# Summing in-degrees beside a bitonic merge sort instead of after it, in a two-part graph network

## The chip, the cores and the metric

The kernel runs on one NeuronCore of a Trainium2 chip. The engines that matter are TensorE (PE, matmuls; its weight loads are the row PEld), VectorE (DVE), ScalarE (ACT), GpSimd (POOL) and the queues that issue DMAs (SP above all). Each has its own stream of instructions and they meet only at semaphores. The metric is the device time of one execution in microseconds (us).

## The reference, cut to what matters

A graph of 12,500 nodes and 412,500 edges (an edge list sorted by destination) goes through a two-layer graph convolution and then through a mesh network with two message steps. The convolution needs, for every node, the sum of the weights of the edges that end in it:

```python
def _gcn_conv(x, row, col, edge_w, W, b, num_nodes):
    ...                                   # self loops of weight 1 are added to row, col, edge_w
    deg = jax.ops.segment_sum(ew, c, num_segments=num_nodes)
    dis = jnp.where(deg > 0, jax.lax.rsqrt(deg), 0.0)
    norm = dis[r] * ew * dis[c]
    msg = (x @ W.T)[r] * norm[:, None]
    return jax.ops.segment_sum(msg, c, num_segments=num_nodes) + b

x = _layernorm(x + gcn2(relu(gcn1(x))))
x = _layernorm(x + mesh_gnn(x, edge_attr, src, dst))   # two steps of edge and node networks
```

`deg` is what this case is about. The mesh network also needs the plain number of edges into each node, so the kernel sums two rows at once: the weights and ones.

## The kernel before

The edges lie in 405 groups of K = 8 columns of 128 edges. Since they are sorted by destination, all destinations of a group fall in a window of W = 64 nodes that starts at the group's first destination, `base_row[g]`. A sum over a group is therefore eight small matmuls: a one-hot of 128 edges by 64 places, times a 128 by 2 tile `wt` of weights and ones, added up in PSUM to a 2 by 64 result, which DVE then adds to the row pair `deg` at the place `base_row[g]`. That place is read by DVE's sequencer from memory into a register before each addition (`values_load`).

The program has these stages, in order of time:

1. Preparation (to 79 us): destinations relative to the groups' bases go to DRAM as `rel_d`; edge lists are loaded.
2. The sort (79 to 792 us). Each of 128 partitions holds a row of RL = 3328 edges and sorts it by source, so that the convolution can later read its table in order. It is a merge network of 78 stages (`stage`, two nested loops over p and c). In a stage, `exchange` (lines 234 to 241) gives DVE three two-input operations over up to 1664 pairs, L237 (a mask of who is larger, written to PSUM), L238 (minimum) and L239 (maximum), and then two predicated copies of the carried weights, L240 and L241. Stages with a remainder have two or three such sets; there are 104 in all. ACT copies the weights over first (L248) and copies the keys that a stage doesn't touch (L244). PE and POOL do nothing here.
3. The sorted rows are split into parts and turned by PE (792 to 822 us).
4. The in-degrees (822 to 1267 us): `edge_loop` runs three times over 135 groups. Per group DVE builds the whole one-hot (128 by 512) in one operation (L385), PE does the eight matmuls (L397), DVE loads the place (L401) and adds (L405). The result is written to DRAM (L691) and read back in another shape (L695) for the reciprocal square root.
5. Two rounds of messages of the convolution (to 4890 us), then the mesh network (to the end), where POOL gathers rows by indirect DMAs.

`spread_degrees` and other `spread_` functions are a slow path for graphs whose windows are wider; for this graph their loops run zero times, at the price of the loop's entry alone. Where `manual_schedule` is used, instructions stay in the order in which they are written; elsewhere a planner sets the order on each engine.

Of the kernel before, what the change touches and what calls it, by code (L numbers as in the profile page):

```python
# [9 lines left out]
F32 = mybir.dt.float32  # L10
I32 = mybir.dt.int32
BF16 = mybir.dt.bfloat16
AF = mybir.ActivationFunctionType
OP = mybir.AluOpType
AX = mybir.AxisListType
ET = mybir.EngineType

NP = 125
P = 128
K = 8  # L20
W = 64
D = 64
GB = 135
SI, DR = 81, 45
R, LA = 5, 3
GI = 5
# [11 lines left out]
def gcn_then_mesh_gnn_kernel(ctx: ExitStack, tc: tile.TileContext, a: dict, out: bass.AP):  # L38
# [23 lines left out]
    NB = N // NP  # L62
    NT = a["dstT"].shape[1]
    NG = NT // K
    TB, IT = GB * K, NG // GB
    TI, ITS = GI * K, NG // GI
    NACC = N + NR
    CB = 4
    NCH = NB // CB
    CN = CB * NP  # L70
    KP = K // 2
    assert N == NB * NP and NB == NCH * CB and NT == IT * TB == ITS * TI

    dram = ctx.enter_context(tc.tile_pool(name="dram", bufs=1, space=bass.MemoryType.DRAM))
    const = ctx.enter_context(tc.tile_pool(name="const", bufs=1))
# [62 lines left out]
    nc.vector.memset(ones, 1.0)  # L138
    base_row = const.tile([1, NG], I32, name="base_row")
    span_row = const.tile([1, ITS], I32, name="span_row")  # L140
    trips = const.tile([1, 6], I32, name="trips")
    rbase_row = const.tile([1, NR], I32, name="rbase_row")
    x1 = const.tile([NP, NB, F], F32, name="x1")

    with tc.tile_pool(name="prep", bufs=2) as prep:
        ldst = prep.tile([P, NT], I32, name="ldst", bufs=1)
        nc.sync.dma_start(ldst, a["dstT"])
        for g0 in range(0, NG, P):
            n = min(P, NG - g0)
            gi = prep.tile([P, K * P], I32, name="gi")  # L150
            nc.sync.dma_start(gi[:n], a["dstG"][g0:g0 + n, :])
            gf = prep.tile([P, K * P], F32, name="gf")
            nc.vector.tensor_copy(gf[:n], gi[:n])
            st = prep.tile([P, 3], F32, name="st")
            nc.vector.tensor_reduce(st[:n, 0:1], gf[:n], axis=AX.X, op=OP.min)
            nc.vector.tensor_reduce(st[:n, 1:2], gf[:n], axis=AX.X, op=OP.max)
            nc.vector.tensor_sub(st[:n, 2:3], st[:n, 1:2], st[:n, 0:1])
            nc.sync.dma_start(base_f[g0:g0 + n, :], st[:n, 0:1])
            nc.sync.dma_start(span_f[g0:g0 + n, :], st[:n, 2:3])

            gr = prep.tile([P, 2, KP, P], BF16, name="gr")
            nc.vector.tensor_scalar(gr[:n].rearrange("g h j e -> g j h e"),
                                    gf[:n].rearrange("g (j h e) -> g j h e", h=2, e=P),
                                    st[:n, 0:1], None, op0=OP.subtract)
            nc.sync.dma_start(relg_d[g0:g0 + n].rearrange("g h c -> g (h c)"),
                              gr[:n].rearrange("g h j e -> g (h j e)"))
        base_bc = prep.tile([P, NG], F32, name="base_bc", bufs=1)
        nc.sync.dma_start(base_bc, base_f.rearrange("g o -> o g").to_broadcast([P, NG]))
        rows = prep.tile([1, 2, NG], F32, name="rows", bufs=1)
        nc.sync.dma_start(rows[:, 0, :], base_f.rearrange("g o -> o g"))  # L170
        nc.sync.dma_start(rows[:, 1, :], span_f.rearrange("g o -> o g"))
        nc.vector.tensor_copy(base_row, rows[:, 0, :])
        mspan = prep.tile([1, ITS], F32, name="mspan", bufs=1)
        nc.vector.tensor_reduce(mspan, rows[:, 1, :].rearrange("o (i g) -> o i g", g=GI),
                                axis=AX.X, op=OP.max)
        nc.vector.tensor_scalar_add(span_row, mspan, 1.0)

        most = prep.tile([1, 1], F32, name="most", bufs=1)
        tf = prep.tile([1, 4], F32, name="tf", bufs=1)

        mins = prep.tile([1, NCH, 2], F32, name="mins", bufs=1)
        nc.gpsimd.iota(mins[:, :, 1], pattern=[[CN, NCH]], base=CN, channel_multiplier=0,
                       allow_small_or_imprecise_dtypes=True)
        nc.vector.memset(mins[:, :, 0], float(N))
        for c in range(NCH):
            if last_group[c] < NG - 1:
                nc.vector.tensor_reduce(mins[:, c:c + 1, 0], rows[:, 0, last_group[c] + 1:], axis=AX.X, op=OP.min)
        nc.vector.tensor_tensor(mins[:, :, 0], mins[:, :, 0], mins[:, :, 1], op=OP.is_ge)
        held = prep.tile([1, 1], F32, name="held", bufs=1)
        nc.vector.tensor_reduce(held, mins[:, :, 0], axis=AX.X, op=OP.min)  # L190
        nc.vector.tensor_reduce(most, rows[:, 1, :], axis=AX.X, op=OP.max)
        nc.vector.tensor_scalar(tf[:, 0:1], most, float(W), held, op0=OP.is_lt, op1=OP.mult)
        nc.vector.tensor_scalar(tf[:, 2:3], tf[:, 0:1], -1.0, 1.0, op0=OP.mult, op1=OP.add)
        nc.vector.tensor_scalar_mul(tf[:, 1:2], tf[:, 2:3], float(ITS))
        nc.vector.tensor_scalar_mul(tf[:, 3:4], tf[:, 0:1], float(IT))
        nc.vector.tensor_copy(trips[:, 0:2], tf[:, 0:2])
        nc.vector.tensor_copy(trips[:, 4:6], tf[:, 2:4])
        dstrel = prep.tile([P, NT], F32, name="dstrel", bufs=1)
        nc.vector.tensor_copy(dstrel, ldst)
        rel3 = dstrel.rearrange("p (g k) -> p g k", k=K)  # L200
        nc.vector.tensor_tensor(rel3, rel3, base_bc[:, :, None].to_broadcast([P, NG, K]), op=OP.subtract)
        nc.sync.dma_start(rel_d, dstrel)
# [7 lines left out]
    with tc.tile_pool(name="sort", bufs=1) as sp, \  # L210
# [1 line left out]
        keys = [sp.tile([NR, RL], F32, name=f"key{i}") for i in range(2)]  # L212
        vals = [sp.tile([NR, RL], F32, name=f"val{i}") for i in range(2)]
        st = sp.tile([NR, 3], F32, name="rst")
        ki = sp.tile([NR, RL], I32, name="ki")
        kj = sp.tile([NR, RL], I32, name="kj")
        mask = pp.tile([NR, RL // 2], I32, name="mask")
        k, other = keys

# [71 lines left out]
            for move in moves:  # L291
                move()

        p, turn = 1, 0
        while p < RL:
            c = p
            while c:
                stage(p, c, keys[turn], keys[1 - turn], vals[turn], vals[1 - turn])
                turn, c = 1 - turn, c // 2
            p *= 2  # L300
        k, free = keys[turn], keys[1 - turn]
        tiles = lambda t: t.rearrange("r (j e) -> r j e", e=P)

# [38 lines left out]
        for t, to in ((free, slot_t), (k, drel_t), (vals[turn], ew_t)):  # L342
            for j0 in range(0, NS, 4):
                n = min(4, NS - j0)
                pt = pp.tile([128, 512], F32, name="ps_st", bufs=2)
                for j in range(n):
                    nc.tensor.transpose(pt[:, j * NR:(j + 1) * NR], tiles(t)[:, j0 + j, :], ident)
                nc.scalar.copy(to[:, j0:j0 + n, :], pt[:, :n * NR].rearrange("e (j r) -> e j r", r=NR))
# [34 lines left out]
    def one_hot(pool, drl, g):  # L383
        oh = pool.tile([P, K, W], F32, name="oh")
        nc.vector.tensor_tensor(oh, iow[:, None, :].to_broadcast([P, K, W]),  # L385
                                drl[:, g * K:(g + 1) * K, None].to_broadcast([P, K, W]), op=OP.is_equal)
        return oh
# [31 lines left out]
    def trip_count(i, most):  # L419
        return nc.values_load(trips[0:1, i:i + 1], min_val=0, max_val=most,  # L420
                              skip_runtime_bounds_check_because="all or none")

    def edge_loop(pool, body):

        with tc.For_i(0, trip_count(5, IT)) as it:
            drl = pool.tile([P, TB], F32, name="drl", bufs=1)
            nc.sync.dma_start(drl, rel_d[:, ds(it * TB, TB)])
            offs = pool.tile([1, GB], I32, name="offs")
            nc.vector.tensor_copy(offs, base_row[0:1, ds(it * GB, GB)])
            body(it, drl, offs)  # L430

    def spread_loop(pool, body, acc, r0, m, which=1):

# [71 lines left out]
    with tc.tile_pool(name="gcn", bufs=1) as gp, tc.tile_pool(name="gcnw", bufs=2) as gw:  # L505
# [19 lines left out]
        nc.sync.dma_start(w2t, a["W2T"])  # L525
        b1 = column(gp, "b1", a["L0_gnn_b1"])
        b2 = column(gp, "b2", a["L0_gnn_b2"])
        nc.vector.memset(deg, 0.0)

        def weights(pool, it, n):  # L530
            ew = pool.tile([P, n], F32, name="ew")
# [3 lines left out]
        def weights_and_ones(pool, it, n):  # L535
            wt = pool.tile([P, n, 2], F32, name="wt")
            nc.vector.tensor_copy(wt[:, :, 0], weights(pool, it, n))
            nc.vector.memset(wt[:, :, 1:2], 1.0)
            return lambda t: [wt[:, t, :]]

        def degrees(it, drl, offs):
            val = weights_and_ones(dw, it, TB)
            for g in range(GB):
                window_sum(one_hot(dw, drl, g), offs, g, lambda k: val(g * K + k), deg, 0, 2)

        with tc.tile_pool(name="degrees", bufs=2) as dw:
            edge_loop(dw, degrees)

        def weigh(xg, ew, g):
            nc.vector.tensor_mul(xg, xg, ew[:, g * K:(g + 1) * K, None].to_broadcast([P, K, F]))  # L550
# [102 lines left out]
                    fold_up(*folds.pop(0))  # L653

        def spread_degrees():
            with tc.tile_pool(name="spread", bufs=2) as sw:
                def body(it, group):
                    val = weights_and_ones(sw, it, TI)
                    for g in range(GI):
                        group(g, val)  # L660
                    return val

                spread_loop(sw, body, deg, 0, 2)

        def spread_messages(table):
            with tc.tile_pool(name="spread", bufs=2) as sw:
# [21 lines left out]

        spread_degrees()

        nc.sync.dma_start(deg_d, deg[:, :2 * NBK * P])  # L691
        by_block = lambda row: row.rearrange("o (b p) -> (o b) p", p=P)
        d = gp.tile([2 * NBK, P], F32, name="d")
        pos = gp.tile([2 * NBK, P], F32, name="pos")
# [618 lines left out]
```

## Time and profile before

| | us |
|---|---|
| median of 15 runs | 15397.31 |
| lowest and highest of them | 15358.05, 15450.96 |
| the profiled execution, its own time | 15461.96 |
| its span | 15460.2 |
| the sort in it | 79 to 792 |
| the in-degrees in it | 822.5 to 1267.5 |

The profile is of one execution, 65 us above the median of the runs. Its page gives busy time by engine; "idle before" is how long the engine stood still just ahead of an instruction, with what ended it. The share of busy time over the whole span says little here, since the stages have different limits; each has to be read for itself. Records of POOL are rough. A small letter q behind an engine's name marks its sequencer, which loads registers, waits and issues DMAs while the engine itself may be busy.

### The profile page before, as it was taken

The numbers are of one execution on the slowest core, as the hardware profiler recorded it, in microseconds if no ns is written. First come the engines' busy times: TensorE is split into PE (matmuls) and PEld (weight loads), VectorE is DVE, ScalarE is ACT, GpSimd is POOL, SyncE is SP. The second block draws the span as 40 slices with busy tenths as digits, with TensorE's granted clock in tenths as the row PEclk, the third lists the DMA queues.
The fourth block names the chain that finished last, engine by engine and source line by source line (L and its number), as shares of the span: only waits on it lengthen the run. The fifth ranks groups of instructions, "written<-read, shape, count | busy, mean of one in ns | idle before, by whom it ended". The sixth has DMA issues, their size and how long they took to land. (4 is left out here: it accounts for less than half of the span.)

```text
span 15460.2 us, 272960 instructions
## 1 busy us (share of the span) xinstructions
PE 11395.6 (74%) x104538; PEld 8580.0 (55%) x104539; DVE 8750.2 (57%) x22373; ACT 2375.2 (15%) x3731; POOL 6370.9 (41%) x6741
## 2 busy tenths in 40 slices
PE   0089999999998788888888888885655556565565
PEld 0078999789997455555455555553444444444443
DVE  9977777677777455555455455453444444444444
ACT  3400000000001222222222222221111111111111
POOL 0000000000001555556565556555666666666664
PEclk9999999899997688888788878787777777777777
DMA  0001111121111222222222222222222222222222
GB/s 28 0 15 54 66 66 66 48 69 66 65 65 47 57 60 61 59 60 62 56 61 60 58 60 62 56 60 58 60 60 60 60 61 60 61 61 60 60 59 50
DMA packets 958543, 871.49 MB, mean 56 GB/s; under 512 B 599416, under 2 KB 706192, under 8 KB 956548
## 3 DMA queue, kind: packets, MB, share of 16 engines
q1 hardware_dynamic: 258034, 493.54, 9.7%
q0 software_dynamic: 207360, 212.75, 7.8%
q10 hardware_dynamic: 491796, 147.08, 4.1%
q8 instruction: 859, 14.07, 0.4%
q14 instruction: 494, 4.05, 0.1%
HBM read 718.12 MB, written 134.51 MB: 55 GB/s over the span
## 5 line engine op out<-in xcount | busy, mean ns | idle before, releaser
L415 POOL DMA_INDIRECT pg<-tab_p,si x6480 | 6277.9, 969 | 3973.9 <-issue 1698.8
L1052 PE MATMUL ps_o<-eb_w,h 128*128 128x128 f32 x6480 | 1381.2, 380 | 1850.2 <-ACT h L1045 1640.2
L1052 PEld LDWEIGHTS ps_o<-eb_w,h 128*128 128x128 f32 x6480 | 1176.1, 272 | 2107.7 <-ACT h L1045 1778.1
L607 PE MATMUL ps_h<-t,roh 128*128 128x112 bf16 (+1 forms) x39936 | 2132.1, 211 | 65.9 <-DVE roh L583 65.9
L607 PEld LDWEIGHTS <-roh 128*128 128x128 bf16 x39936 | 2011.3, 98 | 115.3 <-issue 112.0
L789 POOL MEMSET zero<- 64x192 bf16 x1 | 0.3, 251 | 4015.9 <-DVE agg L639 4015.9
L1116 DVE TENSOR_SCALAR ot<-rb,iop 128x512 bf16<-128x512 bf16 x810 | 294.3, 363 | 2359.0 <-DMA rb<-relg_d 1482.3
L623 PE MATMUL ps_seg<-ohd,msg 128*112 128x112 f32 (+1 forms) x13312 | 1618.2, 266 | 0.0
L474 DVE TENSOR_REDUCE var<-sq 128x8 f32<-128x512 f32 (+2 forms) x1290 | 842.9, 666 | 1266.4 <-issue 717.9
L397 PE MATMUL ps_seg<-oh,y 128*64 128x64 f32 x19440 | 1297.1, 255 | 210.0 <-issue 187.7
L623 PEld LDWEIGHTS ps_seg<-ohd,msg 128*112 128x112 f32 (+1 forms) x13312 | 1407.4, 173 | 0.5
L397 PEld LDWEIGHTS ps_seg<-oh,y 128*64 128x64 f32 x19440 | 1140.2, 166 | 375.0 <-issue 340.6
L614 DVE TENSOR_TENSOR msg<-ps_h,wm 128x448 f32<-128x448 f32 (+1 forms) x1536 | 975.3, 635 | 460.9 <-PE ps_h L607 455.1
L1040 PE MATMUL ps_h<-e,eb_w 128*128 128x512 f32 x1620 | 1183.6, 814 | 62.6 <-issue 34.9
L611 DVE TENSOR_TENSOR ohd<-ior,rdrel 128x448 f32<-128x448 f32 (+1 forms) x1536 | 1011.2, 659 | 234.8 <-PE ps_seg L623 234.8
L473 ACT ACTIVATE sq<-ps_o 128x512 f32<-128x512 f32 (+1 forms) x1240 | 735.2, 593 | 2547.9 <-remote 688.0
L1045 ACT ACTIVATE h<-ps_h,eb_b 128x512 f32<-128x512 f32 x810 | 556.7, 687 | 3098.2 <-remote 1979.7
L1040 PE MATMUL ps_h<-ot,qd 128*128 128x512 bf16 x2430 | 783.7, 424 | 104.0 <-issue 91.3
L479 DVE TENSOR_TENSOR y<-ps_o,rs_y 128x512 f32<-128x512 f32 x1215 | 802.7, 689 | 88.2 <-issue 4.6
L385 DVE TENSOR_TENSOR oh<-iow,drl 128x512 f32<-128x512 f32 x1215 | 830.0, 683 | 14.9 <-DMA drl<-rel_d 7.8
L1042 PE MATMUL ps_h<-ident,pg 128*128 128x128 f32 x3240 | 604.9, 298 | 311.8 <-issue 222.3
L1052 PE MATMUL ps_o<-ee_w,h 128*128 128x128 f32 x3240 | 631.8, 355 | 211.4 <-ACT h L1033 206.4
(280 smaller groups left out, 11573.6 us busy)
## 6 DMA issues: line engine op xcount, KB each, us to landing
mod<-mod_d SPq DMA_DIRECT2D x256, 832.0 KB
pg<-tab_p,si POOLq DMA_INDIRECT x6480
e_d<-e SPq DMA_DIRECT2D x405, 256.0 KB
e<-e_d SPq DMA_DIRECT2D x405, 256.0 KB
rb<-relg_d ACTq DMA_DIRECT2D x1612, 64.0 KB
qd<-tab_q ACTq DMA_DIRECT2D x1612, 24.0 KB
at<-in_attrT SPq DMA_DIRECT2D x405, 32.0 KB
tab_q<-tabs SPq DMA_DIRECT2D x50, 187.5 KB
```

The costliest lines, as they stand in the source:

```text
L385: nc.vector.tensor_tensor(oh, iow[:, None, :].to_broadcast([P, K, W]), drl[:, g * K:(g + 1) * K, None].to_broadcast([P, K, W]), op=OP.is_e ...
L397: nc.tensor.matmul(ps[r:r + n, :W], v, oh[:, k, :], start=(k == 0), stop=(k == K - 1))
L415: nc.gpsimd.indirect_dma_start(out=to[:, k, :], out_offset=None, in_=table, in_offset=bass.IndirectOffsetOnAxis(ap=idx[:, k:k + 1], axis=0))
L473: nc.scalar.activation(sq, o.rearrange("p (k f) -> p k f", f=D), AF.Square, scale=D ** -0.5)
L474: nc.vector.tensor_reduce(v[:, i:i + k], sq, axis=AX.X, op=OP.add)
L479: nc.vector.tensor_tensor(y, o, r[:, i:i + k, None].to_broadcast(list(y.shape)), op=OP.mult)
L607: nc.tensor.matmul(pg[:, (j - j0) * sb * F:(j - j0 + 1) * sb * F], ohs[h][:, u, at * P:(at + 1) * P], t3[:, i, u, b:b + sb * F], start=(i ...
L611: nc.vector.tensor_tensor(ohd[:, :n, :], ior[:, None, :].to_broadcast([P, n, LR]), drel[:, j0:j0 + n, r:r + 1].to_broadcast([P, n, LR]), o ...
L614: nc.vector.tensor_tensor(msg[:, :n * sb * F].rearrange("p (j s f) -> p j s f", s=sb, f=F), pg[:, :n * sb * F].rearrange("p (j s f) -> p j ...
L623: nc.tensor.matmul(acc[:sb * F, :LR], msg[:, j * sb * F:(j + 1) * sb * F], ohd[:, j, :], start=(j0 + j == packs[0][0]), stop=((j0, n, sb) ...
L1040: nc.tensor.matmul(ph, w, v, start=(i == 0), stop=False)
L1052: nc.tensor.matmul(po[:, j * 128:(j + 1) * 128], h[:, j * P:(j + 1) * P], w1, start=False, stop=(j == KP - 1))
```

## The change

The in-degrees are no longer summed after the sort but in pieces along with its stages. Before stage i + 2 of the sort, DVE adds the sums of the six groups of piece i; after stage i is written out, POOL and PE are given piece i: POOL makes the one-hots, now as eight separate operations of 128 by 64 per group with the column of destinations as a scalar operand, and PE does the same matmuls as before, into a PSUM tile with four buffers. There are 68 pieces for 78 stages. POOL also makes the weight tile and clears `deg`. `deg` shares its memory with the two integer buffers of the sort, which are used only before and after the stages. PE, DVE, ACT and POOL now follow the written order during the sort. The loop over groups after the sort is gone; two short conditional loops for the slow path are new.

```diff
-        ki = sp.tile([NR, RL], I32, name="ki")
-        kj = sp.tile([NR, RL], I32, name="kj")
+        big = sp.tile([NR, NACC], F32, name="big")
+        ki, kj = (big[:, i * RL:(i + 1) * RL].bitcast(I32) for i in range(2))
+        deg = big[0:2, :]
...
+        def degrees(i):
+            gs = range(i * GD, min((i + 1) * GD, NG))          # GD = 6
+            for n, g in enumerate(gs):
+                if g % DR == 0:                                # DR = 45
+                    cols = slice(g * K, (g + DR) * K)
+                    drl = sp.tile([P, DR * K], F32, name="drl", bufs=2)
+                    nc.sync.dma_start(drl, rel_d[:, cols])
+                    ew = sp.tile([P, DR * K], F32, name="dew", bufs=2)
+                    nc.sync.dma_start(ew, a["ewT"][:, cols])
+                    wt = sp.tile([P, DR * K, 2], F32, name="wt", bufs=2)
+                    nc.gpsimd.tensor_copy(wt[:, :, 0], ew)
+                    nc.gpsimd.memset(wt[:, :, 1:2], 1.0)
+                    parts[g // DR] = drl, wt
+                drl, wt = parts[g // DR]
+                at = g % DR * K
+                oh = sp.tile([P, K, W], F32, name="doh", bufs=3)
+                for k in range(K):
+                    nc.gpsimd.tensor_scalar(oh[:, k, :], iow, drl[:, at + k:at + k + 1], None, op0=OP.is_equal)
+                if n == 0:
+                    sums[i] = pp.tile([128, 512], F32, name="ps_st", bufs=4)
+                for k in range(K):
+                    nc.tensor.matmul(sums[i][0:2, n * W:(n + 1) * W], wt[:, at + k, :], oh[:, k, :],
+                                     start=(k == 0), stop=(k == K - 1))
+
+        def add_degrees(i):
+            ps = sums.pop(i)
+            for n, g in enumerate(range(i * GD, min((i + 1) * GD, NG))):
+                at = nc.values_load(base_row[0:1, g:g + 1], engines=[ET.DVE], min_val=0, max_val=N, ...)
+                w = deg[:, ds(at, W)]
+                nc.vector.tensor_add(w, w, ps[0:2, n * W:(n + 1) * W])
+
+        p, turn, at_stage, parts_of = 1, 0, 0, -(-NG // GD)
+        with tc.manual_schedule(engines={ET.PE, ET.DVE, ET.Activation, ET.Pool}):
+            nc.gpsimd.memset(deg, 0.0)
+            while p < RL:
+                c = p
+                while c:
+                    if 0 <= at_stage - 2 < parts_of:
+                        add_degrees(at_stage - 2)
+                    stage(p, c, keys[turn], keys[1 - turn], vals[turn], vals[1 - turn])
+                    if at_stage < parts_of:
+                        degrees(at_stage)
+                    turn, c, at_stage = 1 - turn, c // 2, at_stage + 1
+                p *= 2
+        nc.sync.dma_start(deg_d, deg[:, :2 * NBK * P])
...
-        nc.vector.memset(deg, 0.0)
...
-        def degrees(it, drl, offs):
-            val = weights_and_ones(dw, it, TB)
-            for g in range(GB):
-                window_sum(one_hot(dw, drl, g), offs, g, lambda k: val(g * K + k), deg, 0, 2)
-
-        with tc.tile_pool(name="degrees", bufs=2) as dw:
-            edge_loop(dw, degrees)
...
         def spread_degrees():
+            with tc.For_i(0, trip_count(4, 1)):
+                nc.vector.memset(deg, 0.0)
...
+            with tc.For_i(0, trip_count(4, 1)):
+                nc.sync.dma_start(deg_d, deg[:, :2 * NBK * P])
...
-        nc.sync.dma_start(deg_d, deg[:, :2 * NBK * P])
```

More of the change, by code (lines that the diff above doesn't have):

```diff
@@ L22 @@
 D = 64
-GB = 135
+GM = 405
+GD = 6
 SI, DR = 81, 45
@@ L64, in gcn_then_mesh_gnn_kernel @@
     NG = NT // K
-    TB, IT = GB * K, NG // GB
     TI, ITS = GI * K, NG // GI
@@ L71, in gcn_then_mesh_gnn_kernel @@
     KP = K // 2
-    assert N == NB * NP and NB == NCH * CB and NT == IT * TB == ITS * TI
+    assert N == NB * NP and NB == NCH * CB and NT == ITS * TI
     dram = ctx.enter_context(tc.tile_pool(name="dram", bufs=1, space=bass.MemoryType.DRAM))
@@ L140, in gcn_then_mesh_gnn_kernel @@
     span_row = const.tile([1, ITS], I32, name="span_row")
-    trips = const.tile([1, 6], I32, name="trips")
+    trips = const.tile([1, 5], I32, name="trips")
     rbase_row = const.tile([1, NR], I32, name="rbase_row")
@@ L178, in gcn_then_mesh_gnn_kernel @@
         most = prep.tile([1, 1], F32, name="most", bufs=1)
-        tf = prep.tile([1, 4], F32, name="tf", bufs=1)
+        tf = prep.tile([1, 3], F32, name="tf", bufs=1)
         mins = prep.tile([1, NCH, 2], F32, name="mins", bufs=1)
@@ L194, in gcn_then_mesh_gnn_kernel @@
         nc.vector.tensor_scalar_mul(tf[:, 1:2], tf[:, 2:3], float(ITS))
-        nc.vector.tensor_scalar_mul(tf[:, 3:4], tf[:, 0:1], float(IT))
         nc.vector.tensor_copy(trips[:, 0:2], tf[:, 0:2])
-        nc.vector.tensor_copy(trips[:, 4:6], tf[:, 2:4])
+        nc.vector.tensor_copy(trips[:, 4:5], tf[:, 2:3])
         dstrel = prep.tile([P, NT], F32, name="dstrel", bufs=1)
@@ L292, in stage @@
                 move()
[L294 to L300, printed above, removed]
+        sums, parts = {}, {}
+        def degrees(i):
[21 more added lines that the diff above has]
+                                     start=(k == 0), stop=(k == K - 1))
@@ new lines, in add_degrees @@
+        def add_degrees(i):
+            ps = sums.pop(i)
+            for n, g in enumerate(range(i * GD, min((i + 1) * GD, NG))):
+                at = nc.values_load(base_row[0:1, g:g + 1], engines=[ET.DVE], min_val=0, max_val=N,
+                                    skip_runtime_bounds_check_because="a destination is a node's number or N")
+                w = deg[:, ds(at, W)]
+                nc.vector.tensor_add(w, w, ps[0:2, n * W:(n + 1) * W])
+        p, turn, at_stage, parts_of = 1, 0, 0, -(-NG // GD)
@@ L301, in gcn_then_mesh_gnn_kernel @@
+        assert at_stage >= parts_of + 2
+        nc.sync.dma_start(deg_d, deg[:, :2 * NBK * P])
         k, free = keys[turn], keys[1 - turn]
@@ L344, in gcn_then_mesh_gnn_kernel @@
                 n = min(4, NS - j0)
-                pt = pp.tile([128, 512], F32, name="ps_st", bufs=2)
+                pt = pp.tile([128, 512], F32, name="ps_st", bufs=4)
                 for j in range(n):
@@ L421, in trip_count @@
                               skip_runtime_bounds_check_because="all or none")
[L423 to L430, printed above, removed]
     def spread_loop(pool, body, acc, r0, m, which=1):
@@ L1276 @@
     nb = n // NP
-    ng = -(-src.shape[0] // (GB * K * P)) * GB
+    ng = -(-src.shape[0] // (GM * K * P)) * GM
     nt = ng * K
```

## The prediction

> **What bounds the kernel now.** I read the busy time in stretches first, since only the first 1270 us are touched. Its columns are the stretch, its length, then busy time of PE, PEld, DVE, ACT and POOL with instruction counts, the granted clock, DMA share and GB/s.
>
> ```profile
> 79.00:792.00 713.00, 0.00 (x0) 0.00 (x0) 711.27 (x522) 283.12 (x264) 0.00 (x0) 1.00 0.00 0
> 822.50:1267.50 445.00, 401.73 (x6480) 358.03 (x6480) 344.37 (x822) 0.00 (x0) 0.33 (x2) 0.95 0.05 14
> ```
>
> The sort is DVE and nothing else (711 of 713 us); PE and POOL are empty. The in-degrees are PE (402 of 445 us) with DVE close behind. Nothing of the second stretch runs beside the first, so moving it can free up to 445 us, if the sort doesn't grow. The groups by line of the first 1200 us show what the sort is made of (busy us, mean ns, idle before):
>
> ```profile
> L241 DVE COPY_PREDICATED val<-mask,val 128x1664 f32<-128x1664 int32 (+34 forms) x104 | 183.7, 1767 | 0.0
> L240 DVE COPY_PREDICATED val<-mask,val 128x1664 f32<-128x1664 int32 (+34 forms) x104 | 182.6, 1756 | 0.7
> L237 DVE TENSOR_TENSOR mask<-key 128x1664 int32<-128x1664 f32 (+34 forms) x104 | 136.4, 1312 | 0.1
> L238 DVE TENSOR_TENSOR key<-key 128x1664 f32<-128x1664 f32 (+33 forms) x104 | 136.2, 1310 | 0.9
> L239 DVE TENSOR_TENSOR key<-key 128x1664 f32<-128x1664 f32 (+33 forms) x104 | 136.1, 1308 | 0.0
> ```
>
> Over half of it, 408.7 of 775 us, are operations with two SBUF inputs (the keys); the copies take one input from SBUF and the mask from PSUM. That distinction decides the case, because of what the timeline shows where POOL and DVE compute together, in the node encoder (start, duration, instruction):
>
> ```profile
> 4942.15 0.67 POOL L372 TENSOR_TENSOR tabs_r<-tabs_r,tabs 125x256 f32<-125x256 f32 x1
> 4942.33 0.51 DVE L460 TENSOR_TENSOR rs_t<-rs_y 125x4 f32<-125x4 f32 x1
> 4942.87 0.16 DVE L461 SCALAR_TENSOR_TENSOR rs_t<-rs_t,var 125x4 f32<-125x4 f32 x1
> ...
> 4951.66 0.40 POOL L369 CAST tabs<-tabs 125x256 bf16<-125x256 f32 x1 [8.36 <-DMA tab_q<-tabs]
> 4951.82 0.25 DVE L462 SCALAR_TENSOR_TENSOR rs_y<-rs_t,rs_y 125x4 f32<-125x4 f32 x1
> 4952.14 0.67 POOL L370 TENSOR_TENSOR tabs_r<-tabs,tabs 125x256 f32<-125x256 f32 x1
> 4952.18 0.42 DVE L479 TENSOR_TENSOR ny<-ps_o,rs_y 125x256 f32<-125x256 f32 x1
> ```
>
> A DVE operation on four elements that starts inside a POOL operation takes 0.51 or 0.25 us in place of 0.16, and ends within 0.02 us of POOL's end. L479, with one input from PSUM, takes its usual 0.42. Another one-input operation, L457 at 4941.82, was held as well (0.27 against 0.17), so the rule isn't only the number of inputs; what had PSUM among its operands was never held. The other way round, in the edge network:
>
> ```profile
> 5999.25 0.94 POOL L415 DMA_INDIRECT pg<-tab_p,si  x1 [0.30 <-issue]
> ...
> 6003.22 0.68 DVE L385 TENSOR_TENSOR oh<-iow,drl 128x512 f32<-128x512 f32 x1
> 6003.46 1.26 POOL L415 DMA_INDIRECT pg<-tab_p,si  x1 [2.02 <-remote]
> ```
>
> POOL's 0.94 becomes 1.26 beside the two-input L385. Over the whole trace, 2025 gathers overlap no DVE operation and have a median of 0.94 us; 475 overlap L385 alone and have 1.26. So a POOL operation and a DVE operation with two SBUF inputs exclude each other here. The sort's predicated copies, with their mask in PSUM, I take to be free, as L479 is.
>
> **What goes.** From the end of the preparation at 822.5 to the read of the degrees at 1267.35 lie 445 us. In their place stand three skipped loops where one was entered (one skipped loop costs about 2.2 us: the last addition ends at 1260.0, the write is issued at 1262.25), 6.6 us, and the eleven small loads that are issued there anyway (822.8 to 829.2, 6.4 us). Gain: 432 us. The write to DRAM (5 us until it is read) moves under the last stages, as does the clearing of `deg` (L528, 10.6 us on DVE; POOL's is not on DVE's path).
>
> **What DVE gets.** 405 additions, each with a register load. The sequencer's rows for L401 and L405:
>
> ```profile
> L401 DVEq TENSOR_LOAD <-offs x405: 297/301/316, 841.3 to 1258.8; - x135
> L405 DVE TENSOR_TENSOR agg<-agg,ps_seg x405: 207/208/211, 844.1 to 1259.8; 2x64 f32 x135
> ```
>
> Before, L385's 0.67 us hid the load. Now six follow each other: 0.30 load, 0.07 register arithmetic (the sequencer's row FUSED_REGOPS of L405), some 0.15 of gaps between them as the timeline has it, 0.52 each; the next load starts as the addition starts. The first load of six hides under a copy, so five at 0.52 and 0.21: 2.8 us a stage, 190 us over 68 stages if DVE sets the pace. DVE then needs 376 (the two-input share of 713) + 336 + 190 = 902: alone, that would be a gain of 432 - 190 = 242.
> The Trainium skill (DMA: Bandwidth & Descriptors, Latency and other measured facts) gives a register load a floor of about 600 ns. The trace has half of that; by the page the additions would cost about 0.82 each, 4.3 us a stage, still below the bound found next.
>
> **What POOL gets.** 3240 operations of 128 by 64. No row shows this one. One-input rows: CAST at 256 elements 0.397, the affine select at 128 elements 0.282, so 0.9 ns an element and 0.167 fixed: 0.225 at 64, and 0.19 apart, since the next started 0.03 before the end. The two-input row (L372, 256 elements, 0.667) with the same fixed part gives 0.29. The one-hot has one tensor and one column. I take 0.25 apart, between them, and keep 0.19 and 0.33 (0.29 and a tenth more for starting anew behind DVE) as ends.
> The Trainium skill (GPSIMD Engine Reference, Performance pitfalls) says that each small read command costs about 102 cycles that do not overlap the one before. As an estimate from that page, a column read would add 0.085 to the 0.19, some 0.28, and the forecast below would be about 100 us later. No run here shows it.
>
> **The sum.** 48 operations a piece are 12.0 us; DVE's two-input share of a stage is 376/78 = 4.8 us, and these exclude each other: 16.8 us a stage. DVE alone would need 4.8 + 4.3 + 2.8 = 11.9. So POOL plus the excluded share is the bound, and DVE waits for sums ahead of the first addition. POOL may start at 66.6 (last cast of the shared buffer) + 10.6 (clearing) + 0.9 (weight tile) = 78. To its last one-hot: 3240 × 0.25 = 810, nine weight tiles 8, two-input work of some 69 stages 333. Then the last matmuls and additions, 4, and nine stages that have no more additions behind them, 713 × 9/78 = 82, taken as 87 since late ones are full. The sort ends at 78 + 810 + 8 + 333 + 4 + 87 = 1320, not 792: 528 us later. Less 432: 96 us slower, 15461.96 to 15558. The medians lie 65 us lower: 15397 + 96, said as 15495.
>
> PE isn't the bound: a group took 0.98 us, the first ones 1.6; six are 5.9 to 9.6 us, under 16.8. ACT: 283 us of 713, its 3 us copy lies beside the additions and L237 to L239. The planner's freedom is lost on DVE: before, next-stage operations were moved ahead of copies; the waits that this filled are bounded by ACT's 3.6 us a stage, hidden at 16.8. SP: 18 loads and the write, queued behind nothing that DVE waits for.
>
> **Rivals.**
> - A, faster: a one-hot at 0.19 apart. 3240 × 0.06 = 194 less: 98 us gain, 15300. For it: the one-input line of two rows. Against: the column operand, and fresh starts. It turns at 0.22 us an operation, where 528 falls to 432.
> - B, faster still: POOL slips through without stretching anything. Then DVE paces with 190 us more, or POOL with 810 + 8 + 91 + 78 - 792, about 195: about 240 gained, 15160. Against: the held rows above, both ways.
> - C, much slower: POOL's queue never lets DVE in between two of its operations, so DVE's two-input work waits for whole bursts until PSUM buffers run out; then copies and additions no longer overlap one-hots. 7.1 us more a stage (4.3 + 2.8), 68 × 7.1 = 480: 15980. If only the copies are excluded as well, 4.3 × 68 = 292: 15790. For it: POOL's operations overlap by 0.03 back to back. Against: L385 gets in between gathers, and L479 is free.
> - D: the change doesn't take work off the path, as PE's matmuls are late anyway. Excluded by PE's 5.9 to 9.6 us against 16.8.
>
> **How the numbers follow.** My forecast, 0.22 to 0.33 us a one-hot under exclusion: 0.60, 15397 to 15755. A 0.15, B 0.11, C 0.14. The range leaves out the last part of B and of C: 15200 to 15960. A measurement can tell about 0.2%, 31 us. Faster by more: B, most of A, 0.25. Within: the edge between A and the forecast, 0.07. Slower: 0.68.
>
> **What would show it.** POOL's one-hots start about 0.25 us apart while DVE copies, and only one or two fit around each of L237 to L239, whose records lengthen by 0.1 to 0.3 us; DVE stands idle some 4 us ahead of the first addition of most stages, released by PE or POOL; the sort ends near 1320; nothing after it changes but its place. I am wrong if DVE is never idle there (A or B) or if POOL runs 48 in a row while a two-input operation stands still (C).

## The result and the profile after

The changed kernel takes 16028.09 us (median of 9 runs) against 15408.11 us for the kernel before (46 runs): 1.040 times as long, 95% interval 1.0385 to 1.0414, or 620 us more. The profiled execution has a span of 15959.1 us, 499 us above the one before; the rest of the difference between the medians lies in how these two spans stand to their medians (before: 52 us above, after: 69 us below). At the read of the in-degrees the profile after is already 599 us behind (1865.85 against 1267.35); what follows came out 100 us shorter in it (14093 against 14193), in the mesh network, at a granted clock of 0.79 there against 0.78.

Busy time in two stretches of the kernel after, the sort and what lies between it and the read of the in-degrees (columns as in the prediction: PE, PEld, DVE, ACT, POOL, granted clock, DMA share, GB/s):

```profile
81.00:1820.00 1739.00, 1210.78 (x6480) 280.03 (x6480) 798.16 (x927) 278.73 (x264) 1648.30 (x3256) 1.00 0.01 2
1820.00:1866.00 46.00, 10.82 (x78) 10.30 (x78) 25.39 (x23) 10.13 (x21) 0.33 (x2) 0.81 0.06 21
```

The sort was DVE without a gap in 713 us. It is now POOL without a gap until 1729 us, with DVE busy for less than half of the 1739 us (798). The second stretch is the gain: 46 us, where before there were 476 from the end of the sort (791.4) to the read at 1267.35. So 430 us were taken away, and the sort grew from 791 to 1820, by 1029. Then the groups from 60 to 2000 us (busy us, mean ns, idle before):

```profile
L315 POOL TENSOR_SCALAR doh<-iow,drl 128x64 f32<-128x64 f32 x3240 | 1644.8, 528 | 0.0
...
L319 PEld LDWEIGHTS ps_st<-doh,wt 128*2 128x2 f32 x6480 | 280.0, 82 | 1449.1 <-POOL doh L315 1449.1
...
L241 DVE COPY_PREDICATED val<-mask,val 128x1664 f32<-128x1664 int32 (+34 forms) x104 | 180.5, 1736 | 0.0
L240 DVE COPY_PREDICATED val<-mask,val 128x1664 f32<-128x1664 int32 (+34 forms) x104 | 179.2, 1723 | 0.0
L237 DVE TENSOR_TENSOR mask<-key 128x1664 int32<-128x1664 f32 (+34 forms) x104 | 132.9, 1278 | 1.1 <-issue 0.2
L239 DVE TENSOR_TENSOR key<-key 128x1664 f32<-128x1664 f32 (+34 forms) x104 | 132.4, 1273 | 0.0
L238 DVE TENSOR_TENSOR key<-key 128x1664 f32<-128x1664 f32 (+34 forms) x104 | 132.3, 1272 | 0.0
L328 DVE TENSOR_TENSOR big<-big,ps_st 2x64 f32 x405 | 84.6, 209 | 939.8 <-PE ps_st L319 832.6 <-DVE big L328 107.2
```

POOL's 3240 one-hots have no idle time before them at all; DVE's idle time, 940 us, lies before the additions, 833 of it waiting for PE, and PE's weight loads wait for POOL (1449 us). The sort's own operations did not get longer (1312, 1308 and 1310 ns before). One line on the one-hots gives minimum, median and maximum of their durations in ns:

```profile
L315 POOL TENSOR_SCALAR doh<-iow,drl x3240: 430/430/5932, 78.3 to 1728.9; 128x64 f32<-128x64 f32 x191
```

Alone, a one-hot takes 430 ns, and the next starts 410 ns after it (3148 of 3239 spacings). The long ones are those that run into L237 to L239. From the timeline, POOL and DVE around 140 us:

```profile
137.66 8.60 POOL L315 TENSOR_SCALAR doh<-iow,drl 128x64 f32<-128x64 f32 x8
```

```profile
137.35 0.21 DVE L328 TENSOR_TENSOR big<-big,ps_st 2x64 f32 x1 [0.31 <-DVE big L328]
137.87 0.21 DVE L328 TENSOR_TENSOR big<-big,ps_st 2x64 f32 x1 [0.31 <-DVE big L328]
138.01 1.88 DVE L237 TENSOR_TENSOR mask<-key 128x1664 int32<-128x1664 f32 x1
139.81 1.87 DVE L238 TENSOR_TENSOR key<-key 128x1664 f32<-128x1664 f32 x1
141.62 1.87 DVE L239 TENSOR_TENSOR key<-key 128x1664 f32<-128x1664 f32 x1
143.42 1.89 DVE L240 COPY_PREDICATED val<-mask,val 128x1664 f32<-128x1664 int32 x1
145.22 1.88 DVE L241 COPY_PREDICATED val<-mask,val 128x1664 f32<-128x1664 int32 x1
```

Eight one-hots that would need 3.3 us take 8.6 here: one of them, started at 138.07, takes 5.73 us and ends 0.3 us after L239 (143.49), and the others run at 0.41 beside the copies. In the whole sort 83 one-hots are stretched like this. Until POOL is done there are 69 runs of such operations (of three, or of six where a stage has two sets); in 60 of them a single one-hot spans the run to its end, and in nine a one-hot ended inside the run and the next one was held in its turn.

The time of the last one-hot then adds up: 78.3 (the first) + 3240 × 0.410 = 1329 + nine weight tiles 8 + time shut out 314 = 1729. The 314 is what the other terms leave; counted by itself, what the 83 stretched one-hots take beyond 430 ns each is 315. The last additions and the nine stages that follow them bring the sort to 1820.

### The profile page after: what moved, and what is told of

It is laid out like the page before. It is cut to its first block, busy times and chain, and to the rows that moved or that the text cites. A ratio compares the mean times of both kernels' runs of the same rounds, so it can differ in the third digit from the quotient of the medians.

```text
span 15959.1 us, 275489 instructions
## 1 busy us (share of the span) xinstructions
PE 12127.9 (76%) x104538; PEld 8468.7 (53%) x104539; DVE 8493.0 (53%) x21957; ACT 2368.7 (15%) x3731; POOL 8045.8 (50%) x10000
## 5 line engine op out<-in xcount | busy, mean ns | idle before, releaser
L315 POOL TENSOR_SCALAR doh<-iow,drl 128x64 f32<-128x64 f32 x3240 | 1644.8, 528 | 0.0
L319 PE MATMUL ps_st<-doh,wt 128*2 128x64 f32 x6480 | 1210.8, 290 | 518.9 <-POOL doh L315 403.7
L319 PEld LDWEIGHTS ps_st<-doh,wt 128*2 128x2 f32 x6480 | 280.0, 82 | 1449.1 <-POOL doh L315 1449.1
```

Of the source, the lines that this page charges most:

```text
L315: nc.gpsimd.tensor_scalar(oh[:, k, :], iow, drl[:, at + k:at + k + 1], None, op0=OP.is_equal)
L319: nc.tensor.matmul(sums[i][0:2, n * W:(n + 1) * W], wt[:, at + k, :], oh[:, k, :], start=(k == 0), stop=(k == K - 1))
```

## The experiments

They ran on two other chips, on which the kernel before takes 15953 us (there ran: without the column, half the width, one in eight, and the first run with the one-hots on DVE) and 13441 us (there ran the other four). The difference lies in the mesh network, which takes 11.0 and 8.6 ms there at granted clocks of 0.76 and 0.85; the sort doesn't feel it (the same kernel ended it at 1091.8 and 1091.5 us). So I compare where the sort ends within the profile, and ratios only between kernels on one chip. The kernel after didn't run on these two chips; its 1820 us are from the first one. Five of the kernels ran only once, and of those only the profile is read.

My theory after the result: the sum in the prediction has the right form (one-hots plus the excluded share of DVE) and one wrong price, 0.41 us in place of 0.25. The rivals: POOL is slow only because DVE works beside it; the wait is the lag of the additions or PE, not POOL; adding along with the sort is a loss in itself.

The trace of the kernel after settles the first rival. At 625.1 us DVE ends its copies and then waits until 639.83; from 629.49 on, POOL makes one-hots while DVE does nothing:

```profile
639.83 0.21 DVE L328 TENSOR_TENSOR big<-big,ps_st 2x64 f32 x1 [14.69 <-PE ps_st L319]
```

```profile
629.49 10.69 POOL L315 TENSOR_SCALAR doh<-iow,drl 128x64 f32<-128x64 f32 x26
```

That is 25 spacings of 0.41 and one duration. Over the whole sort 1969 spacings fall into times in which DVE did nothing, and their median is 0.410; the 715 beside the copies L240 and L241 alone have 0.410 too. So a one-hot takes 0.41 us by itself.

### Without the column operand

```diff
-                    nc.gpsimd.tensor_scalar(oh[:, k, :], iow, drl[:, at + k:at + k + 1], None, op0=OP.is_equal)
+                    nc.gpsimd.tensor_scalar(oh[:, k, :], iow, float(k), None, op0=OP.is_equal)
```

> The column of destinations is replaced by a fixed number, so the one-hots and with them the in-degrees are not those of the graph; count, width and everything else stay. My theory: the length of the sort is 78 us + 3240 times the spacing of two one-hots (0.41 us in the changed kernel) + some 310 us in which two-input DVE work shuts POOL out + some 95 us of stages without additions. If reading the column as an operand is what makes 0.41 of my 0.25, the spacing falls to 0.2 to 0.33 us and the sort ends 260 to 680 us earlier than 1820. If the column costs nothing, the spacing stays 0.41 and the end at 1820. Rival (POOL is slow because DVE works beside it): spacing stays 0.41 whatever the operands are.

```profile
L315 POOL TENSOR_SCALAR doh<-iow x3240: 361/368/5888, 79.7 to 1706.1; 128x64 f32<-128x64 f32 x191
```

The duration falls from 430 to 368 ns, the sort ends at 1797. But the spacing has two values: 0.326 us for the numbers 0, 1 and 2, and 0.447 for 3 to 7, so that the mean, 0.403, hardly moves and neither forecast holds cleanly. Each number has its fixed place among the eight one-hots of a group, so the run doesn't tell the number from the place. If the three short ones are taken as the price without a column, the column is worth 0.084 us (0.410 - 0.326); what the other five cost instead, the trace doesn't say. By the mean it is 0.007.

### Half the width

```diff
-                    nc.gpsimd.tensor_scalar(oh[:, k, :], iow, drl[:, at + k:at + k + 1], None, op0=OP.is_equal)
+                    nc.gpsimd.tensor_scalar(oh[:, k, :W // 2], iow[:, :W // 2], drl[:, at + k:at + k + 1], None, op0=OP.is_equal)
...
-                    nc.tensor.matmul(sums[i][0:2, n * W:(n + 1) * W], wt[:, at + k, :], oh[:, k, :],
+                    nc.tensor.matmul(sums[i][0:2, n * W:n * W + W // 2], wt[:, at + k, :], oh[:, k, :W // 2],
...
-                w = deg[:, ds(at, W)]
-                nc.vector.tensor_add(w, w, ps[0:2, n * W:(n + 1) * W])
+                w = deg[:, ds(at, W // 2)]
+                nc.vector.tensor_add(w, w, ps[0:2, n * W:n * W + W // 2])
```

> One-hots, matmuls and additions cover only the first 32 of 64 places of each window, so the in-degrees are not complete; the counts of instructions stay. If a one-hot's price is mostly a fixed start, the spacing stays near 0.38 us or more and the sort ends no earlier than about 1720. If it is by element, the spacing falls to 0.2 to 0.28 us and the sort ends at 1150 to 1400. At the 0.9 ns an element of the casts in the kernel before it would fall by 0.03 us only.

```profile
L315 POOL TENSOR_SCALAR doh<-iow,drl x3240: 352/353/5933, 77.9 to 1480.4; 128x32 f32<-128x32 f32 x191
```

The spacing falls to 0.332 us and the sort ends at 1571, 249 us earlier; 3240 × 0.078 = 253. So 32 elements cost 0.078 us: 2.4 ns an element, 0.156 for 64, and 0.254 is left as a start, the column's share in it (0.084 by the run above). That lies between the two forecasts: the start is the larger part of the 0.410, but an element costs nearly three times the 0.9 ns of the casts. POOL's pace moves the end of the sort one to one.

### An addition in place of the comparison

```diff
-                    nc.gpsimd.tensor_scalar(oh[:, k, :], iow, drl[:, at + k:at + k + 1], None, op0=OP.is_equal)
+                    nc.gpsimd.tensor_scalar(oh[:, k, :], iow, drl[:, at + k:at + k + 1], None, op0=OP.add)
```

> The comparison becomes an addition with the same column, so the in-degrees are wrong; count, width and operands stay. If comparing is what makes 2.4 ns an element out of the casts' 0.9, the spacing of two one-hots falls by up to 0.1 us, to 0.31, and the sort ends near 1500. If not, 0.41 and 1820.

```profile
L315 POOL TENSOR_SCALAR doh<-iow,drl x3240: 432/432/5920, 81.3 to 1739.8; 128x64 f32<-128x64 f32 x191
```

The spacing stays at 0.412 us, the sort ends at 1831. It isn't comparing that costs 2.4 ns an element.

### Two wide operations in place of eight narrow ones

```diff
-                for k in range(K):
-                    nc.gpsimd.tensor_scalar(oh[:, k, :], iow, drl[:, at + k:at + k + 1], None, op0=OP.is_equal)
+                nc.gpsimd.tensor_tensor(oh, iow[:, None, :].to_broadcast([P, K, W]),
+                                        drl[:, at:at + K, None].to_broadcast([P, K, W]), op=OP.subtract)
+                nc.gpsimd.tensor_single_scalar(oh, oh, 0.0, op=OP.is_equal)
```

> POOL makes a group's one-hots in two wide operations, a difference of 128 by 512 and a comparison with zero over 512, in place of eight of 128 by 64; the output is unchanged. If a one-hot is a start of 0.17 us, a column read of 0.08 and 2.4 ns an element, the two cost 0.13 + 512 x 2.1 ns = 1.2 us and 0.17 + 512 x 2.4 ns = 1.4 us, 2.6 us a group in place of 3.28; 405 x 0.68 = 275 us less, so the sort ends near 1545. Rival (the price is by instruction): two in place of eight would end it near 1000, where DVE sets the pace.

```profile
L314 POOL TENSOR_TENSOR doh<-iow,drl x405: 1034/1044/6405, 79.6 to 1413.3; 128x512 f32<-128x512 f32 x135
```

```profile
L316 POOL TENSOR_SCALAR doh<-doh x405: 1487/1488/3119, 83.6 to 1418.3; 128x512 f32<-128x512 f32 x135
```

2.59 us a group from start to start, as expected (2.6), and the sort ends at 1512 (1545 expected). The wide comparison is priced by its elements: 1.454 apart at 512 against 0.326 at 64 is 2.5 ns an element. Fewer starts help, but POOL still needs 1047 us for 405 groups before it is shut out at all.

### More of DVE's work with two inputs in SBUF

```diff
-        mask = pp.tile([NR, RL // 2], I32, name="mask")
+        mask = sp.tile([NR, RL // 2], I32, name="mask")
```

> The mask of the exchanges moves from PSUM to SBUF, so that the predicated copies L240 and L241 too have two inputs from SBUF; nothing else changes. If POOL is shut out by DVE work with two SBUF inputs, it is now shut out by the copies as well: stretched one-hots cover runs of five DVE operations, some 300 us more are lost (the copies' 336 us over some 69 of 78 stages), POOL's last one-hot ends near 2030 and the sort near 2115. Rival (POOL is slow by itself and the stretched records are only late reports): both stay where they were, 1729 and 1820, within what the copies' own price changes.

Groups of this kernel, 78 to 2200 us:

```profile
L315 POOL TENSOR_SCALAR doh<-iow,drl 128x64 f32<-128x64 f32 x3240 | 1934.7, 617 | 0.0
...
L241 DVE COPY_PREDICATED val<-mask,val 128x1664 f32<-128x1664 int32 (+34 forms) x104 | 180.5, 1736 | 0.0
L240 DVE COPY_PREDICATED val<-mask,val 128x1664 f32<-128x1664 int32 (+34 forms) x104 | 179.4, 1725 | 0.0
```

```profile
L315 POOL TENSOR_SCALAR doh<-iow,drl x3240: 430/430/13172, 80.4 to 2020.9; 128x64 f32<-128x64 f32 x191
```

The copies cost DVE what they cost before, yet the sort ends at 2112 (2115 expected), POOL's last one-hot at 2021 instead of 1729, and the one-hots are busy for 290 us more. The spacing of undisturbed ones stays 0.410. This shows the exclusion by itself: the same DVE time, with its second input in SBUF rather than PSUM, shuts POOL out. The rival of this run, that the stretched records are only late reports, falls.

### One one-hot in eight

```diff
-                for k in range(K):
-                    nc.gpsimd.tensor_scalar(oh[:, k, :], iow, drl[:, at + k:at + k + 1], None, op0=OP.is_equal)
+                nc.gpsimd.tensor_scalar(oh[:, 0, :], iow, drl[:, at:at + 1], None, op0=OP.is_equal)
...
-                    nc.tensor.matmul(sums[i][0:2, n * W:(n + 1) * W], wt[:, at + k, :], oh[:, k, :],
+                    nc.tensor.matmul(sums[i][0:2, n * W:(n + 1) * W], wt[:, at + k, :], oh[:, 0, :],
```

> POOL makes one of the eight one-hots of a group and the eight matmuls all read it, so the in-degrees are wrong; matmuls, additions and the order stay. My theory: POOL then needs 405 x 0.41 = 166 us and DVE sets the pace: the sort's 713 us plus 190 us for the additions, so the sort ends near 982 and the run is 220 to 250 us faster than the kernel before (about 15165). Rival (PE or the two-stage lag of the additions is what DVE waits for): DVE still stands idle ahead of the additions and the sort ends well above 1050.

Waits of DVE from 78 to 1100 us, the first line (total us, times, longest):

```profile
DVE big L327 <- DVE big L327: 84.9, 269, 0.7
```

The sort ends at 959 (982 expected); the kernel takes 0.984 of the time of the kernel before on that chip (interval 0.979 to 0.988). DVE no longer waits for PE ahead of an addition, only for the register load between two of them. The 6480 matmuls, unchanged in number, keep PE busy for 465 us here (402 in the kernel before), so most of the 1211 in the kernel after are not time that they need. Neither PE nor the two-stage lag holds DVE up, and 168 us (959 - 791) is what the 405 additions cost: 0.41 each, the first of six being hidden.

### One-hots back on DVE, sums beside the sort

```diff
-                for k in range(K):
-                    nc.gpsimd.tensor_scalar(oh[:, k, :], iow, drl[:, at + k:at + k + 1], None, op0=OP.is_equal)
+                nc.vector.tensor_tensor(oh, iow[:, None, :].to_broadcast([P, K, W]),
+                                        drl[:, at:at + K, None].to_broadcast([P, K, W]), op=OP.is_equal)
...
-                    if 0 <= at_stage - 2 < parts_of:
-                        add_degrees(at_stage - 2)
+                    for n in range(GD):
+                        if at_stage < parts_of:
+                            degrees(at_stage, n)
+                        if 0 <= at_stage - 2 < parts_of:
+                            add_degrees(at_stage - 2, n)
                     stage(p, c, keys[turn], keys[1 - turn], vals[turn], vals[1 - turn])
-                    if at_stage < parts_of:
-                        degrees(at_stage)
```

Both functions now take one group at a time, and the one-hots have six buffers.

> One part undone: the one-hots go back to DVE, one operation of 128 by 512 per group as before the change, each put ahead of one addition so that the addition's register load hides behind it; one-hot buffers six instead of three; sums and additions stay beside the sort. My theory: six times 0.83 us (one-hot to addition 0.69, addition to one-hot 0.14) is 5.0 us a stage more on DVE and nothing waits for POOL: 68 x 5.0 = 340 us more sort, 432 less after it, about 90 us faster than the kernel before (15320). Rival (adding the in-degrees along with the stages is a loss by itself, by lost order or PE): no faster than before.

> The same kernel as the one with its one-hots back on DVE, timed in more rounds. From its first profile the sort ends 300 us later than before and the read of the in-degrees comes 130 us earlier; 0.99 of the kernel before, 110 to 170 us faster.

The timeline of the second of these two runs, DVE around 304 us:

```profile
302.29 1.96 DVE L241 COPY_PREDICATED val<-mask,val 128x1664 f32<-128x1664 int32 x1
304.15 0.67 DVE L314 TENSOR_TENSOR doh<-iow,drl 128x512 f32<-128x512 f32 x1
304.75 0.20 DVE L329 TENSOR_TENSOR big<-big,ps_st 2x64 f32 x1
304.88 0.67 DVE L314 TENSOR_TENSOR doh<-iow,drl 128x512 f32<-128x512 f32 x1
305.48 0.20 DVE L329 TENSOR_TENSOR big<-big,ps_st 2x64 f32 x1
```

A pair of one-hot and addition takes 0.73 us; the register load hides behind the one-hot, and DVE waits for it 2.2 us in the whole sort. The sort ends at 1092, 300 us later than before (340 expected, at 0.83 a pair), and the read of the in-degrees comes at 1138, 129 us earlier. It takes 0.990 (0.987 to 0.993) of the kernel before on the one chip and 0.991 (0.989 to 0.993; 13322 against 13441 us) on the other. This version is faster than the kernel before, and its sort ends 728 us earlier than that of the kernel after. Moving the in-degrees beside the sort is a gain of about 1%; giving their one-hots to POOL is what made it a loss of 4%. Besides the engine of the one-hots, their place between the additions and the number of their buffers differ from the kernel after. There DVE waited only 107 us between additions, and POOL never stood idle for a buffer, so neither can have moved the end of the sort by 728 us.

## Why the prediction was wrong

The direction was right and the mechanism was the one forecast; the time, 15495 with a range to 15960, was too low.

- **The step that failed is the price of a one-hot** in "What POOL gets": 0.25 us apart, with 0.33 as the upper end. It is 0.41. That is 3240 × 0.16 = 518 us too little, and the sort ended 500 later than forecast (1820, not 1320); the time shut out, 314 instead of 333, makes up the rest. With 0.41 in its place the same sum gives 15397 + 96 + 518 = 16011, where 16028 was measured, so the form of the sum holds. I had taken 0.9 ns an element from a line through one point each of two other operations, a cast and the affine select; the half-width run gives 2.4, which is 0.10 of the missing 0.16. Start and column together are 0.25, where I had 0.13 and some 0.06 for the second operand; how these split, the runs leave open. No row of the trace showed an operation of this kind. The slowest row, L372, spread over its 256 elements without a fixed part, is 2.6 ns each, 0.167 for 64; with the fixed 0.167 on top this is 0.33, no more than the upper end that I had. So the spread between the known rows was too narrow a bound for a kind that none of them was.
- The column read was worth 0.084 us by the three short spacings of the run without it, against the estimate of 0.085 that I had worked out from the Trainium skill (GPSIMD Engine Reference, Performance pitfalls). That they agree rests on those three alone; in the other five a fixed number cost 0.037 more than the column, and no run shows that the column is a command of the page's kind. Taken as the estimate that the prediction gave it, some 0.28 in place of 0.25, it would have made up a fifth of the error.
- **The gain**, 432 us, was 430. **The exclusion** was right in kind and size (333 and 314), and the run with the mask in SBUF confirms it. I had it wrong in detail: L237 to L239 were to lengthen by 0.1 to 0.3 us with a one-hot or two fitting around each. Their means did not lengthen, and in 60 of 69 runs of them no one-hot ended before the run did.
- **The additions**: 0.52 us from one to the next was right (136.31, 136.83 and so on in the timeline). DVE alone would have needed the 959 us of the run with an eighth of the one-hots; I had 982 by the same sum (791 + 190). The register load takes 303 ns at the median, not the floor of about 600 that the Trainium skill gives (DMA: Bandwidth & Descriptors, Latency and other measured facts).
- **The wait** ahead of the first addition of a stage, forecast at about 4 us, was 833/68 = 12.2, by the same wrong price (six groups at 48 × 0.16 = 7.7 more).
- **Rival C** has nearly the measured time, 15980, but not its mechanism: one-hots did overlap the copies and additions, and it was POOL that couldn't get between DVE's operations, not the reverse. A and B fall, as the one-hot is far above 0.22 and the exclusion holds.

## What to carry to other kernels

Before work is moved to an idle engine, its price there has to come from an operation of the same kind: here one price, wrong by 0.16 us and taken 3240 times, was nearly the whole error (518 us). An idle POOL beside a DVE that works on two SBUF inputs is idle for only part of the time; its work takes its own time plus all of that DVE time (1329 and 314 us here). And a register load that stood behind other work costs again where the work ahead of it goes: keep one operation between two additions, as the version with pairs at 0.73 us does.

## What the runs showed of the hardware that I had not expected

- A tensor-scalar operation on POOL costs 2.4 to 2.5 ns an element (0.332 us at 32 elements, 0.410 at 64, 1.454 at 512 without a column), while a copy of 360 elements in the same kernel takes 0.494 us. Adding and comparing cost the same.
- With a fixed number as operand, the spacing was 0.326 us for 0, 1 and 2 and 0.447 for 3 to 7, at the same duration of 0.368. What makes the difference, the number or the place in the group, stays open.
- A run of DVE operations with two SBUF inputs mostly isn't interrupted by POOL: in 60 of 69 runs the waiting one-hot ends only 0.3 us or so after the last of three or six (5.7 us in the timeline above), and with the mask in SBUF one record covers up to 13.2 us.
- Moving one input of a DVE operation from PSUM to SBUF left its own time as it was (1736 ns) and took 292 us from POOL.
